# Ranks by odd counts, two sums moved to GpSimd, and a new order in a graph network kernel on one core

## The chip, the cores and the metric

The kernel runs on one core of a Trainium2 chip. The metric is the time of one execution on the device in microseconds (us). TensorE is called PE in the profile, its weight loads PEld, VectorE DVE, ScalarE ACT, GpSimd POOL and SyncE, whose queue issues the transfers, SP.

## The reference

There are 128 graphs of 128 nodes with 64 features, and a matrix `adj` of weights, most of them zero. Two layers follow each other; each adds its result to its input and normalizes over the features.

```
mask = adj > 0                                      # layer 0
diff = x[:, :, None, :] - x[:, None, :, :]
h    = relu((x @ W1a)[:, :, None, :] + diff @ W1b + b1)
hm   = einsum('bjkh,bjk->bjh', h, mask)             # 192 hidden features
deg  = sum(mask, -1)
x    = layernorm(x + hm @ W2 + deg * b2)

m    = relu(relu(x @ W1 + b1) @ W2 + b2)            # layer 1
msg  = relu(adj @ m)
gi, gh = msg @ W_ih.T + b_ih, x @ W_hh.T + b_hh     # three gates of 64
r, z = sigmoid(i_r + h_r), sigmoid(i_z + h_z)
n    = tanh(i_n + r * h_n)
x    = layernorm(x + (1 - z) * n + z * x)
```

The first layer's `hm` sums, for each node, a rectified vector over its neighbours only. A node has few neighbours, so the kernel gathers them.

## The kernel before, in words

The 128 graphs go through in 32 groups of four (`G = 4`). The nodes are in an order that spreads them over two halves of 64 (`K`). For each group the kernel does this:

- **Preparation** (`prep_parts`). `masks` (L410) compares the weights with zero on GpSimd. `ranks` (L416) counts, by a matmul of the mask with a triangle matrix `incl2`, how many marked nodes of the same half stand up to and with each node; L419 multiplies this by the mask on VectorE, so that marked nodes hold their rank 1, 2, 3 and so on, and all others 0. `degrees` and `counts` find how many neighbours a node has and how many extra segments of four (`W1`) it needs beyond the first eight (`W0`). `offsets` (L461, L462) makes `past` and `own`, which say which node owns which extra segment; `turned`, `owners` and `places` carry ranks over to the segments as `place`. `picks` (L518) compares `rankT` with 1 to 8 and `place` with 9 to 12, so that twelve one-hot matrices come out, `pick0` and `pick1`.
- **Values.** `values` multiplies the features by all projections at once; ScalarE copies the result to `uv` (L535). `pieces` splits a part of it into three bf16 pieces. `others` (L474) makes `t4`, the last 64 columns of `uv` times the degree plus `x`, by four VectorE instructions, one for each graph.
- **The main loop.** Each graph has six stretches, four of `pick0` and two of `pick1`, so 24 a group. In each, ScalarE writes the base value to a PSUM buffer `pv` (`seeds`, L581), TensorE adds the gathered values by 12 matmuls (`gathers`, L612), and VectorE sums absolute values into `part` (`reduces`, L628). There are three `pv` buffers. GpSimd adds up `part` (`together`, L650 to L657).
- **The tail** (`tail_parts`): the second matmul and `y0` with `t4` (L292), a normalization, the messages, the gates, the update and the second normalization, much of it on GpSimd.

Every part is a generator that stops between steps. The order is written out by hand: `TIMETABLE` gives each step a number, a group's numbers are shifted by `PER = 768` from the group before, and the steps are recorded in rising order of these numbers. `FIRST` and `SETUP` do this for the first group and the constants. The numbers are ranks in an order, not times. Each engine runs its instructions in the recorded order, and waits at each for what it needs; transfers stand in SP's queue in the same way. `uv`, `rankT` and most prepared tiles have two buffers, `t4` and `maskT` three, the loads four, and one pool of two PSUM buffers, `ps_w`, serves all matmuls but the gathers.

In `setup`, the tiles `gw1` and `gw2` get the second layer's weights on the diagonal of a cleared square. They are cleared by VectorE (L227) in the step that issues their transfers, which stands behind the main loop's first four reductions in the recorded order. The same step issues the transfers of the second layer's biases, which the next step of `setup` (L241 to L245) works on.

Of the kernel before, what the change touches and what calls it, by code (L numbers as in the profile page):

```python
# [12 lines left out]
ALU = mybir.AluOpType  # L13
# [15 lines left out]

PER = 768  # L30
TIMETABLE = {
    "load": (-1520,), "masks": (-771,), "ranks": (-470, -453), "degrees": (-560, -487), "turned": (-31, -23),
    "counts": (-196,), "offsets": (-3, 39, 50, 155, 157, 160, 160), "owners": (467, 555), "places": (193, 214),
    "pieces": (347, 412, 417, 418), "others": (-73, 422, 583, 1355), "values0": (-108, -102, -102),
    "values1": (136, 192, 192), "pick0": (-211, -102, 40, 69, 230, 278, 473, 532), "pick1": (579, 613, 613, 615),
    "over0": (263, 304), "over2": (461, 501), "base0": (-58,), "together0": (810, 990, 990, 1055),
    "sums0": (1213, 1219, 1219), "base1": (809,), "together1": (851, 1112, 1184, 1184), "base2": (594,),
    "together2": (1058, 1131, 1253, 1284), "sums2": (1328, 1348, 1383), "base3": (643,),
    "together3": (1240, 1256, 1316, 1326), "second": (1283, 1403, 1417, 1485, 1485, 1485), "turn": (1485, 1489),
    "message1": (1505, 1508), "message2": (1516, 1540), "message3": (1540, 1631),  # L40
    "gates": (1906, 1931, 1931, 1935, 1960, 1993), "update": (2192, 2539, 2962, 2962, 3012, 3044, 3156, 3920, 4537),
    "seed": (476, 511, 583, 612, 612, 661, 661, 686, 707, 721, 741, 806, 879, 923, 923, 973, 1019, 1065, 1073, 1156,
        1156, 1180, 1193, 1238),
    "gather": (487, 528, 589, 634, 649, 661, 703, 703, 734, 741, 760, 877, 907, 923, 946, 1002, 1034, 1069, 1131,
        1174, 1193, 1220, 1220, 1244),
    "reduce": (574, 574, 640, 647, 680, 706, 709, 736, 778, 803, 817, 914, 961, 1010, 1034, 1034, 1071, 1129, 1145,
        1176, 1214, 1237, 1276, 1322),
}


# [29 lines left out]
def adj_resnorm_kernel(  # L80
# [81 lines left out]
    def setup(ps_g, ps_w):  # L162
        def spread(t, src):
            nc.sync.dma_start(t, src.rearrange("(o n) -> o n", o=1).to_broadcast(list(t.shape)))

        for h in range(2):
            nc.sync.dma_start(wab[h * F : (h + 1) * F], w1.rearrange("(c f) h -> f c h", c=2))
        yield
        nc.vector.memset(bias, 0.0)
        nc.sync.dma_start(w2c, w2.rearrange("(c h) f -> h c f", c=2))  # L170
        for h in range(2):
            spread(bias[h * F : h * F + 3, 0:H], b1)
            spread(bias[h * F : h * F + 3, H:V], b2)
        nc.sync.dma_start(b1c, b1.rearrange("(c h) -> h c", c=2))
        make_identity(nc, ident)
        make_upper_triangular(nc, upper)
        nc.gpsimd.memset(nhalf, -0.5)
        nc.vector.memset(ones_h, 1.0)
        nc.vector.memset(zeros, 0.0)
        nc.vector.memset(halves, 0.0)  # L180
        for h in range(2):
            nc.vector.memset(halves[h * K : (h + 1) * K, h : h + 1], 1.0)
        nc.vector.tensor_copy(ident_h, ident)
        nc.vector.tensor_sub(strict, upper, ident)
        nc.vector.tensor_copy(incl2, upper)
        nc.vector.memset(incl2[0:K, K:N], 0.0)
        nc.vector.tensor_scalar_mul(strict_w, strict, -float(W1))
        nc.vector.tensor_copy(incl, upper)
        at = const.tile([N, 3], F32, name="at")
        nc.vector.tensor_add(at, ident[:, 0:3], ident[:, F : F + 3])  # L190

        for i in range(3):
            p = ps_g.tile([N, 2, 512], F32, tag="g", name="pv")
            for c in range(2):
                nc.tensor.matmul(p[:, c, :], ones_h, zeros, start=True, stop=True)
        ips = ps_w.tile([N, N], F32, tag="w", name="ips")
        nc.tensor.matmul(ips, ones_h, strict, start=True, stop=True)
        yield
        nc.vector.tensor_add(wall[:, 0:H], wab[:, 0, :], wab[:, 1, :])
        nc.vector.tensor_scalar_mul(wall[:, V : V + H], wab[:, 1, :], -1.0)  # L200
        nc.vector.tensor_copy(iota, ips)
        nc.vector.tensor_scalar_mul(w2c, w2c, 0.5)
        yield

        tps = ps_w.tile([HC, 4, F], F32, tag="w", name="tps")
        for c in range(4):
            cs = (V, V + HC, 0, HC)[c]
            nc.tensor.transpose(tps[:, c, :], wall[0:F, cs : cs + HC], ident[0:F, 0:F])
        nc.vector.tensor_copy(wT, tps.rearrange("p c (o f) -> p c o f", o=1).to_broadcast([HC, 4, 2, F]))
        yield  # L210
        dps = ps_w.tile([N, 2, F], F32, tag="w", name="dps")
        for d in range(2):
            for c in range(2):
                nc.tensor.matmul(dps[:, d, :], wT[:, 2 * d + c], w2c[:, c, :], start=c == 0, stop=c == 1)
        cps = ps_w.tile([N, F], F32, tag="w", name="cps")
        for c in range(2):
            nc.tensor.matmul(cps, b1c[:, c : c + 1].to_broadcast([HC, N]), w2c[:, c, :], start=c == 0, stop=c == 1)
        nc.vector.tensor_copy(wall[:, H:V], dps[:, 0, :])
        nc.vector.tensor_copy(wall[:, V + H : 4 * N], dps[:, 1, :])
        nc.vector.tensor_add(bias[:, H:V], bias[:, H:V], cps)  # L220
        yield
        piece = const.tile([N, NBI], BF16, name="piece")
        three_rows(slice(0, V), piece, at)
        yield

        for t, src in ((gw1, g_w1), (gw2, g_w2)):
            nc.vector.memset(t, 0.0)  # L227
            for h in range(2):
                nc.sync.dma_start(t[h * F : (h + 1) * F, h * F : (h + 1) * F], src)
        spread(bi, b_ih)  # L230
        spread(bias[:, V + F : V + 256], b_hh)
        spread(bias[:, V + 256 : NBI], g_b2)
        spread(b2bc, b2)
        for h in range(2):
            hs = slice(h * F, (h + 1) * F)
            nc.sync.dma_start(gb1[hs], g_b1.rearrange("(h o) -> h o", o=1))
            nc.sync.dma_start(wm[hs, 0:F], w_ihT[:, 128:H])
            nc.sync.dma_start(wm[hs, F:H], w_ihT[:, 0:128])
            nc.sync.dma_start(wx[hs, :], w_hhT)
        yield  # L240
        nc.vector.tensor_copy(bias[:, V : V + F], bi[:, 128:H])  # L241
        nc.vector.tensor_add(bias[:, V + F : V + H], bias[:, V + F : V + H], bi[:, 0:128])

        nc.vector.tensor_scalar_mul(bias[:, V + 256 : NBI], bias[:, V + 256 : NBI], 0.5)
        three_rows(slice(V, NBI), piece, at)  # L245
# [133 lines left out]
    with ExitStack() as fast:  # L379
# [25 lines left out]
        def prep_parts(s):  # L405
# [6 lines left out]

            def ranks():

                p = ps_w.tile([N, G, N], F32, tag="w", name=f"pc{g}")
                nc.tensor.matmul(p, incl2, s["maskT"], start=True, stop=True)  # L416
                yield
                s["rankT"] = prep.tile([N, G, N], BF16, tag="rankT", name=f"rankT{g}")
                nc.vector.tensor_mul(s["rankT"], p, s["maskT"])  # L419

            def degrees():
                p = ps_w.tile([N, G, 2], F32, tag="w", name=f"pd{g}")
# [8 lines left out]
            def counts():  # L431
# [5 lines left out]
                s["nseg"] = nseg_all[:, g * G : (g + 1) * G]  # L437
                nc.gpsimd.tensor_scalar(s["nseg"], rnd, BIGR, None, ALU.subtract)
                s["wseg"] = prep.tile([N, G], BF16, tag="wseg", name=f"wseg{g}")
                nc.gpsimd.tensor_scalar(s["wseg"], s["nseg"], float(W1), None, ALU.mult)  # L440
                tot = prep.tile([N, G], F32, tag="tot", name=f"tot{g}")
                nc.gpsimd.tensor_scalar(tot, s["nseg"], 2.0 * W1, 2.0 * W0, ALU.mult, ALU.add)
                s["npad"] = prep.tile([N, G], F32, tag="npad", name=f"npad{g}")
# [26 lines left out]
            def others():  # L470

                s["t4"] = prep.tile([N, G, F], F32, tag="t4", name=f"t4_{g}", bufs=3)
                for i in range(G):
                    nc.vector.scalar_tensor_tensor(  # L474
                        out=s["t4"][:, i, :], in0=s["uv"][:, i, V + H : 4 * N], scalar=s["deg"][:, i : i + 1],
                        in1=s["x"][:, i, :], op0=ALU.mult, op1=ALU.add,
                    )
                    yield

            def turned():  # L480

# [31 lines left out]
            def picks(t):  # L513
                def part():
                    name, n, src, first = ("pick1", W1, "place", W0 + 1) if t else ("pick0", W0, "rankT", 1)
                    s[name] = prep.tile([N, n, G, N], BF16, tag=name, name=f"{name}_{g}")
                    for i in range(n):
                        nc.vector.tensor_scalar(s[name][:, i], s[src], float(first + i), None, ALU.is_equal)  # L518
                        yield

                return part
# [320 lines left out]
```

## Time and profile before

| | |
|---|---|
| median of 3 runs | 1085.34 us (1084.07 to 1085.81) |
| the profiled execution | 1083.69 us |
| its span, from first to last instruction | 1081.8 us |
| its mean granted TensorE clock | 0.974 |
| busy: PE, PEld | 952.1, 778.3 us (88%, 72%) |
| busy: DVE, ACT, POOL | 992.6, 934.4, 840.4 us (92%, 86%, 78%) |
| longest groups: L628 on DVE; L581 on ACT (two forms); L612 on PE | 709.2; 409.3 and 206.3; 499.4 us |

In the table by stretches, a row holds the bounds of the stretch, its length, and for each of PE, PEld, DVE, ACT and POOL the busy time with the number of instructions; then the granted clock, the share of the DMA engines and their rate. A row of waits names an engine and line, what ended its waiting, the sum, how often, and the longest. A row of the timeline has start, duration, engine, line, operation and tiles; in brackets stands the idle time of the engine ahead of it and what ended it. Instructions of one engine overlap a little: one starts while the end of the one before is still written.

### The profile page before, as it was taken

How to read it: one execution, taken by the hardware profiler on the slowest of the kernel's cores; microseconds unless marked ns; L12 is line 12 of the kernel's file. 1: busy time of each engine (PE TensorE's matmuls, PEld its weight loads, DVE VectorE, ACT ScalarE, POOL GpSimd, SP SyncE). 2: the span in 40 equal slices, each digit the busy share in tenths (PEclk: the TensorE clock that was granted, in tenths of full speed). 3: DMA queues.
4: the chain of work that ended last, by engine and by line, in shares of the span. 5: the costliest groups of instructions: out<-in, count | busy, mean ns of one | idle time of the engine just before them, and what ended most of it. 6: DMA issues, size and time to landing. Idle time of an engine off the chain costs nothing.

```text
span 1081.8 us, 33583 instructions
## 1 busy us (share of the span) xinstructions
PE 952.1 (88%) x13432; PEld 778.3 (72%) x13432; DVE 992.6 (92%) x2352; ACT 934.4 (86%) x1576; POOL 840.4 (78%) x1227
## 2 busy tenths in 40 slices
PE   6588999999999999999999999999999998999882
PEld 4367777877777777777777777777777777777761
DVE  6598999999999999999999999999999999999971
ACT  3489999999999999999999999999999999999850
POOL 2266678888888888888888888888888888888766
PEclk9699999999999999999999999999999999999995
DMA  1200000000000000000000000000000000000000
GB/s 49 59 2 22 22 22 21 27 7 26 22 26 26 26 27 7 26 22 27 26 26 26 7 27 21 26 27 26 26 7 26 22 26 27 26 7 6 7 6 22
DMA packets 21368, 23.95 MB, mean 22 GB/s; under 512 B 4050, under 2 KB 17112, under 8 KB 21208
## 3 DMA queue, kind: packets, MB, share of 16 engines
q1 hardware_dynamic: 21208, 21.76, 6.7%
q8 instruction: 107, 1.75, 0.6%
q14 instruction: 53, 0.43, 0.1%
HBM read 17.55 MB, written 4.19 MB: 20 GB/s over the span
## 4 chain that ended last, share of the span: by engine, by line
PE 34%; POOL 25%; DVE 20%; ACT 16%; issue 3%; DMA 1%; SPq 0%; POOLq 0%; ACTq 0%; DVEq 0%
PE pv L612 16%; DVE part L628 13%; ACT pv L581 10%; PE pu L528 4%; POOL part L654 3%; POOL part L657 3%; ACT b L547 3%; POOL rs L275 2%; POOL part L650 2%; DVE pick L518 2%; PE pm L305 2%; PE pa L323 2%; POOL uc L365 2%; POOL ub L362 2%; POOL y L368 2%
## 5 line engine op out<-in xcount | busy, mean ns | idle before, releaser
L628 DVE TENSOR_REDUCE part<-pv 128x192 f32<-128x768 f32 x768 | 709.2, 946 | 21.8 <-PE pv L612 14.9
L612 PE MATMUL pv<-b,pick 64*128 64x192 bf16 x9216 | 499.4, 245 | 65.2 <-ACT pv L581 64.1
L612 PEld LDWEIGHTS <-pick 64*128 64x128 bf16 x9216 | 387.9, 94 | 155.3 <-issue 125.7
L581 ACT COPY pv<-uv 128x768 f32<-128x768 f32 x512 | 409.3, 809 | 37.7 <-DVE part L628 33.7
L581 ACT COPY pv<-us 128x768 f32<-128x768 f32 x256 | 206.3, 806 | 16.8 <-DVE part L628 10.3
L650 POOL TENSOR_TENSOR part<-part 128x384 f32<-128x384 f32 x128 | 127.8, 998 | 76.4 <-DVE part L628 76.2
L535 ACT COPY uv<-pu 128x512 f32<-128x512 f32 x128 | 68.6, 586 | 35.3 <-PE pu L531 35.3
L670 PE MATMUL ph<-ownT,part 128*96 128x128 f32 x512 | 88.3, 274 | 1.2 <-POOL part L657 1.2
L528 PE MATMUL pu<-wall,xT 64*128 64x512 f32 x256 | 86.8, 645 | 1.4 <-ACT off L454 1.2
L556 POOL TENSOR_TENSOR b<-r,b 128x1024 bf16<-128x1024 f32 (+1 forms) x35 | 68.8, 1965 | 20.7 <-ACT b L553 17.4
L518 DVE TENSOR_SCALAR pick<-rankT 128x512 bf16<-128x512 bf16 x256 | 84.1, 330 | 0.0
L654 POOL TENSOR_TENSOR part<-part 128x192 f32<-128x192 f32 x128 | 78.2, 611 | 2.5
L287 PE MATMUL pw<-w2c,hmT 96*128 96x64 f32 x512 | 78.2, 284 | 0.6 <-ACT hmT L676 0.5
L669 PE MATMUL ph<-ident,part 128*96 128x128 f32 x256 | 71.6, 280 | 7.0 <-ACT pv L581 6.7
L468 POOL CAST own<-own 128x512 f32<-128x512 bf16 x32 | 19.5, 610 | 74.5 <-DVE own L462 74.5
L657 POOL TENSOR_TENSOR part<-part 128x192 f32<-128x192 f32 x128 | 77.1, 602 | 0.0
L287 PEld LDWEIGHTS pw<-w2c,hmT 96*128 96x128 f32 x512 | 66.9, 190 | 10.8 <-ACT hmT L676 5.7
L652 POOL TENSOR_TENSOR part<-part 128x192 f32<-128x192 f32 x128 | 74.1, 590 | 0.0
L670 PEld LDWEIGHTS ph<-ownT,part 128*96 128x96 f32 x512 | 70.6, 166 | 2.7 <-POOL part L657 1.8
L275 POOL TENSOR_TENSOR rs<-ve,nhalf 128x4 f32<-128x4 f32 x64 | 66.5, 1039 | 5.3
L592 PE MATMUL pz<-uv,own 128*128 128x192 f32 x256 | 60.0, 358 | 9.4 <-DVE larger L429 9.4
L550 POOL TENSOR_TENSOR r<-uv,b 128x1024 f32<-128x1024 f32 x31 | 66.1, 2131 | 0.0
(137 smaller groups left out, 1626.3 us busy)
## 6 DMA issues: line engine op xcount, KB each, us to landing
adjT<-in_adjT_dram SPq DMA_DIRECT2D x32, 256.0 KB, 2.8
xT<-in_xT_dram SPq DMA_DIRECT2D x64, 64.0 KB, 2.6
x<-in_x_dram SPq DMA_DIRECT2D x32, 128.0 KB, 2.3
out_dram<-o SPq DMA_DIRECT2D x32, 128.0 KB, 1.7
wab<-in_w_dram SPq DMA_DIRECT2D x2, 96.0 KB, 2.5
bi<-in_b_ih_dram SPq DMA_DIRECT2D x1, 96.0 KB
bias<-in_b_hh_dram SPq DMA_DIRECT2D x1, 96.0 KB
wx<-in_w_hhT_dram SPq DMA_DIRECT2D x2, 48.0 KB, 3.5
```

Source lines behind the costliest of these rows:

```text
L275: nc.gpsimd.tensor_tensor(rs, ve, nhalf[:, 0:n], ALU.pow)
L287: nc.tensor.matmul(p[:, i, :], s["hmT"][:, i, c, :], w2c[:, c, :], start=c == 0, stop=False)
L518: nc.vector.tensor_scalar(s[name][:, i], s[src], float(first + i), None, ALU.is_equal)
L528: nc.tensor.matmul(ps[h], s["xT"][ks, i, :], wall[ks, :], start=True, stop=False)
L581: nc.scalar.copy(v, src.rearrange("p (c b h) -> p c b h", c=1, b=1).to_broadcast(list(v.shape)))
L612: nc.tensor.matmul(v[:, h, j, :], pick[ks, a + j, i, :], s[f"b{c}"][ks, i, F : F + H], start=False, stop=c == 2, skip_group_check=True,)
L628: nc.vector.tensor_reduce(into, view(s["pv", i, k]).rearrange("p c b h -> p h c b"), AX.XY, ALU.add, apply_absolute_value=True,)
L650: nc.gpsimd.tensor_tensor(f[:, 0:2], f[:, 0:2], f[:, 2:4], ALU.add)
L652: nc.gpsimd.tensor_tensor(f[:, 0], f[:, 0], f[:, 1], ALU.add)
L654: nc.gpsimd.tensor_tensor(f[:, 0], f[:, 0], f[:, no], ALU.subtract)
L657: nc.gpsimd.tensor_tensor(f[:, 0], f[:, 0], f[:, 1], ALU.add)
L670: nc.tensor.matmul(p[:, i, c, :], s["part1", i0 + i][:, 0, cs], s["ownT"][:, i0 + i, :], start=False, stop=True, skip_group_check=True,)
```

## The change

The triangle matrix gets 2 above the diagonal and 1 on it. The count of a marked node is then 2r - 1 for rank r, and that of any other node is even. So `rankT` needs no mask: ScalarE copies the counts, the picks compare with 1, 3, 5 and so on, and the constants that turn ranks into places are doubled. `others` makes `t4` of four graphs by two GpSimd instructions, a multiply with the degree spread over 64 columns and an add. `gw1` and `gw2` are cleared in the first step of `setup` with work on VectorE. The whole `TIMETABLE` is a new one; `PER`, `SETUP` and `FIRST` stay.

```diff
-    "load": (-1520,), "masks": (-771,), "ranks": (-470, -453), "degrees": (-560, -487), "turned": (-31, -23),
-    "counts": (-196,), "offsets": (-3, 39, 50, 155, 157, 160, 160), "owners": (467, 555), "places": (193, 214),
-    "pieces": (347, 412, 417, 418), "others": (-73, 422, 583, 1355), "values0": (-108, -102, -102),
+    "load": (-1520,), "masks": (-559,), "ranks": (-122, -122), "degrees": (-402, -367), "turned": (-19, -1),
+    "counts": (-114,), "offsets": (-22, -22, 80, 228, 245, 348, 349), "owners": (1039, 1066), "places": (368, 431),
+    "pieces": (337, 538, 550, 595), "others": (1085, 1194), "values0": (-55, -50, -37), "values1": (204, 204, 268),
...
-    "seed": (476, 511, 583, 612, 612, 661, 661, 686, 707, 721, 741, 806, 879, 923, 923, 973, 1019, 1065, 1073, 1156,
-        1156, 1180, 1193, 1238),
+    "seed": (644, 644, 657, 674, 684, 685, 711, 728, 728, 741, 761, 837, 923, 937, 978, 1149, 1149, 1173, 1203, 1221,
+        1271, 1326, 1395, 1397),
...
-        nc.vector.tensor_copy(incl2, upper)
+        nc.vector.scalar_tensor_tensor(out=incl2, in0=strict, scalar=2.0, in1=ident_h, op0=ALU.mult, op1=ALU.add)
         nc.vector.memset(incl2[0:K, K:N], 0.0)
-        nc.vector.tensor_scalar_mul(strict_w, strict, -float(W1))
+        nc.vector.tensor_scalar_mul(strict_w, strict, -2.0 * W1)
...
+        nc.vector.memset(gw1, 0.0)
+        nc.vector.memset(gw2, 0.0)
...
         for t, src in ((gw1, g_w1), (gw2, g_w2)):
-            nc.vector.memset(t, 0.0)
...
-                nc.vector.tensor_mul(s["rankT"], p, s["maskT"])
+                nc.scalar.copy(s["rankT"], p)
...
-                nc.gpsimd.tensor_scalar(s["wseg"], s["nseg"], float(W1), None, ALU.mult)
+                nc.gpsimd.tensor_scalar(s["wseg"], s["nseg"], 2.0 * W1, None, ALU.mult)
...
-                for i in range(G):
-                    nc.vector.scalar_tensor_tensor(
-                        out=s["t4"][:, i, :], in0=s["uv"][:, i, V + H : 4 * N], scalar=s["deg"][:, i : i + 1],
-                        in1=s["x"][:, i, :], op0=ALU.mult, op1=ALU.add,
-                    )
-                    yield
+                nc.gpsimd.tensor_tensor(s["t4"], s["uv"][:, :, V + H : 4 * N], wide(s["deg"], G), ALU.mult)
+                yield
+                nc.gpsimd.tensor_tensor(s["t4"], s["t4"], s["x"], ALU.add)
...
-                        nc.vector.tensor_scalar(s[name][:, i], s[src], float(first + i), None, ALU.is_equal)
+                        nc.vector.tensor_scalar(s[name][:, i], s[src], 2.0 * (first + i) - 1.0, None, ALU.is_equal)
```

## The prediction

> **What bounds the kernel now.** I read the table by stretches first, then the waits of the even part, then the timeline of one period, then the start.
>
> ```profile
> 0.00:54.00 54.00, 30.77 (x232) 20.93 (x234) 31.94 (x92) 21.95 (x42) 14.01 (x31) 0.78 0.20 54
> ...
> 540.00:648.00 108.00, 99.57 (x1440) 82.53 (x1439) 104.26 (x249) 99.04 (x167) 91.01 (x135) 1.00 0.07 22
> ```
>
> The columns are PE, PEld, DVE, ACT, POOL. The eight stretches from 108 to 972 us are alike: VectorE (DVE) is busy 834.6 of 864 us (96.6%), ScalarE (ACT) 796.2 (92.2%), TensorE (PE) 795.3 (92.0%), GpSimd (POOL) 713.7 (82.6%), at a granted clock of 1.00. The long L518 pick that ends each period starts at 499.69 and, four periods on, at 626.02: one group of four graphs takes 31.58 us. In these, DVE works 30.50, ACT 29.10, PE 29.07 and POOL 26.09. VectorE bounds, with 1.08 us idle, but two engines are only 1.4 us behind. The even part reaches from about 54 to 1026 us, 30.8 periods.
>
> The waits of 108 to 972 us (27.4 periods):
>
> ```profile
> ACT pv L581 <- DVE part L628: 33.9, 104, 0.7
> ACT uv L535 <- PE pu L531: 20.1, 28, 0.7
> ...
> DVE rh L350 <- ACT rz L348: 10.8, 27, 0.4
> ...
> DVE part L628 <- PE pv L612: 7.9, 26, 0.6
> ```
>
> ACT's 2.48 us of idle time in a period are 1.24 for a reduction that frees a `pv` buffer, 0.73 for the projection matmul, and 0.5 of small gaps. The three buffers of `pv` tie seed (ACT), gather (PE) and reduction (DVE) together, 24 times a period.
>
> **What VectorE loses.** Durations in a row overlap, so I take the distance from one start to the next.
>
> ```profile
> 504.02 0.67 DVE L419 TENSOR_TENSOR rankT<-pc,maskT 128x512 bf16<-128x512 f32 x1
> 504.61 1.80 DVE L628 TENSOR_REDUCE part<-pv 128x192 f32<-128x768 f32 x2
> ...
> 508.22 0.27 DVE L474 SCALAR_TENSOR_TENSOR t<-uv,deg,x 128x64 f32<-128x64 f32 x1
> 508.41 0.95 DVE L628 TENSOR_REDUCE part<-pv 128x192 f32<-128x768 f32 x1
> ```
>
> The product with the mask costs 0.59, one `t4` instruction 0.19, four 0.78 (the pair at 515.38 takes 0.39 to the next start). 30.50 - 0.59 - 0.78 = **29.13 us** for VectorE.
>
> **What ScalarE gains.** One copy of 128x512 out of PSUM, as `rank` is:
>
> ```profile
> 525.10 0.59 ACT L487 COPY rank<-pr 128x512 bf16<-128x512 bf16 x1
> 525.58 0.39 ACT L317 ACTIVATE m<-pn 128x256 f32<-128x256 f32 x1
> ```
>
> It costs 0.48: 29.10 + 0.48 = **29.58 us**, now the longest of the four. The f32 source bounds it: `place` (f32 to bf16) stands 0.64 from the next start. I take 0.48, the closer row, since the seed behind `place` may have waited. In the new order the count matmul stands right behind gather 23 on PE, and ACT reaches the copy after two seeds, which wait for reductions 21 and 22 (0.87 each), so the matmul (0.39) is hidden. If it is late, the copy holds all later seeds for up to one gather, 0.6 us a period.
>
> **What GpSimd gains.** A multiply with a broadcast operand (L281's form, 0.57 from start to start) and an add of two full ones (L368's, about 0.69): 26.09 + 1.26 = 27.35 us. Nothing waits early: the add stands some 280 of the 768 plan units (11 us) ahead of the `y0` that reads it, and the next load into `x`'s buffer, now freed by GpSimd, a further 360 units later. I cost the wait at nothing; without that cover it is at most 1.3 us a period.
>
> **New period.** ScalarE's 29.58 plus its waits. From below: only the projection wait goes on half as long, 0.35: 29.9. From above: all 2.48 of idle time stays: 32.06. VectorE's release of `pv` is now 0.45 us shorter per period than ScalarE's work and no longer the bound, but reductions still come in runs of three behind picks and statistics. I keep the projection's 0.73 (the first `uv` still stands right behind its matmul, which in the new order also needs the buffer that `mT` frees) and half of the 1.24: 29.58 + 0.73 + 0.62 = **30.93**, 0.65 less. Over 30.8 periods: **-20 us**.
>
> The odd counts and doubled constants change no operation's size; in setup a two-input instruction (0.35, as `own`) replaces a copy (0.22).
>
> **What the order moves.** Mask, counts and first picks of the next group come some 80 to 350 units later (a mask 559 units ahead of its group's zero instead of 771, the rank copy 122 instead of 453), and seeds, gathers and reductions some 170 later, so the distance from preparation to use stays about the same. SP issues the same 4 loads a group at the same place; their buffers' last readers stand hundreds of units ahead. The adding-up of `part`, 26.09 with all else on GpSimd, keeps its number of instructions. I cost these moves at nothing beyond the waits in the next sum; the rivals hold what they may cost.
>
> **The start.**
>
> ```profile
> 28.33 0.31 DVE L227 MEMSET gw<- 128x128 f32 x2
> 28.52 2.38 SPq L229 DMA_DIRECT2D gw<-in_g_w_dram  x4
> ...
> 34.31 0.19 DVE L241 COPY bias<-bi 128x64 f32<-128x64 f32 x1 [5.68 <-DMA bi<-in_b_ih_dram]
> 34.77 0.29 DVE L242 TENSOR_TENSOR bias<-bias,bi 128x128 f32<-128x128 f32 x1 [0.26 <-DMA bias<-in_b_hh_dram]
> ...
> 36.02 0.20 DVE L244 TENSOR_SCALAR bias<-bias 128x64 f32<-128x64 f32 x1 [0.96 <-DMA bias<-in_g_b_dram]
> ```
>
> Clearing the weights' tiles stands behind the fourth reduction in VectorE's order; SP's queue waits for it with the weight, bias and load transfers behind, and VectorE then waits for them. Moved up, the clearing fits into the 0.97 us in which VectorE waits for `wab`, and SP goes on at 9.0 us, as soon as its loads for group 1 are issued. The bias transfers start some 19 us earlier and are there. That removes 5.68 + 0.26 + 0.96 + 0.31 = 7.2 us. Late next is the first reduction behind setup: now it also waits 3.78 us for `pz`, `us`, `ownT` and a seed, and in the new order the second `pz` and `ownT` come later. I take half of that, 1.9: **-9 us**, between -6 and -12.
>
> **The end.** The page's last 56 us are a chain through group 31. In GpSimd's order `ve`, `rs` of group 30 (1.3 us) now stand behind group 31's `y`, not ahead of it, but with `yc` and an `o` still ahead of its last `rs`. I cost it at 0, within 1.5 either way.
>
> **Sum.** From the profiled execution, 1083.69 us (span 1081.8 and 1.9 around it): -20 - 9 gives 1054.7. The median shown, 1085.34, is 1.65 above it, so **1056**.
>
> **A rule that speaks against it.** VectorE's instructions are sometimes longer beside GpSimd's:
>
> ```profile
> 531.18 0.59 DVE L518 TENSOR_SCALAR pick<-rankT 128x512 bf16<-128x512 bf16 x1
> ...
> 1020.09 1.37 DVE L474 SCALAR_TENSOR_TENSOR t<-uv,deg,x 128x64 f32<-128x64 f32 x2
> ```
> ```profile
> 531.03 0.59 POOL L652 TENSOR_TENSOR part<-part 128x192 f32<-128x192 f32 x1
> ...
> 1020.07 0.73 POOL L365 TENSOR_TENSOR uc<-ub,tn 128x256 f32<-128x256 f32 x1
> ```
>
> A pick that is 0.28 elsewhere took 0.59 and ended 0.15 us after the GpSimd addition at its side (531.62); two `t4`, 0.47 elsewhere, took 1.37. So a collision costs 0.31 to 0.45, say 0.38. Today about one pick of twelve per period is hit, as 84.1 us for 256 against a median of 0.284 also says (11.4 us over 32 groups). `past` and `own` run at 0.25 and 0.35, mostly while GpSimd itself waits for `own`.
> The Trainium skill, SBUF — State Buffer, section Who interferes with whom, says that VectorE and GpSimd share a pair of ports under an exclusive lock, taken by fast-mode instructions and those with two SBUF inputs, and that the loser waits for the whole instruction. By that rule, the trace agrees for these two, and the new order, which spreads `past` and `own` beside GpSimd's mask (1.5 us), could pay it more often.
>
> **Rivals.**
> - *The lock eats it* (slower, 0.17). Twenty VectorE instructions of a period can collide (12 picks, 4 `past`, 4 `own`). With six more hits VectorE needs 29.13 + 6 x 0.38 = 31.4, and with today's 1.08 idle 32.5: +0.9 x 30.8 - 9 = +19, 1104. It decides from (1.37 + 9/30.8)/0.38 = 4.4 more hits a period on. For it: GpSimd goes from 83 to 88% of a period. Against: today's twenty-four candidates are hit about once.
> - *ScalarE runs almost without a gap* (0.18): 29.9, -1.68 x 30.8 = -52, with the start 1026. For it: VectorE's own idle time is only 1.08. Against: ScalarE waits on two partners.
> - *The order gives nothing* (0.12): three engines within 0.5 us of each other lose in waiting what VectorE saves; 31.58 stays and only the start counts: 1076. At its worst, with ScalarE's whole 2.48 (32.06), it is 1091; that part is what I count as no difference.
> - *The early clearing frees nothing* (0.05), if another wait holds SP's queue: 1065. The built program shows SP's first weight transfer waiting only for the clearing and an older load, so it is unlikely.
> - My forecast (0.48): periods of 30.4 to 31.4, 1038 to 1071.
>
> **Numbers.** Eight in ten: 1028 to 1092, which leaves out the best of the second rival and most of the first. A measurement of this kernel tells about 0.2% from no change: faster 0.78, within 0.2% 0.05, slower 0.17.
>
> **What would show it.** In the changed profile: ScalarE busiest in the even stretches (above 95%), VectorE about 94%; a period near 30.9; ScalarE's wait for reductions at half of 1.24; no DMA wait at the bias copies; picks still near 284 ns in the median. It is wrong if picks, `past` or `own` are often above 0.5 us, if the rank copy waits for its matmul, or if VectorE idles over 2 us for gathers.

## The result, and the profile after

The changed kernel takes **1053.40 us** (median of 4 runs, 1052.88 to 1053.97) where the kernel before takes 1085.57 (4 runs beside them): a ratio of 0.9702, 95% interval 0.9689 to 0.9715. Forecast were 1056 and faster. The total came out nearly; the table below shows that the gain of the periods was forecast 2.7 us too high and the gain of the start 2.7 us too low, so that the two errors cancelled.

Each group has one `y0` (L292 before, L293 after), so its 32 starts are a clock that counts groups. First and last `y0` in the timelines of VectorE, of the kernel before:

```profile
76.25 0.41 DVE L292 TENSOR_TENSOR y<-pw,t 128x256 f32<-128x256 f32 x1
...
1053.56 0.42 DVE L292 TENSOR_TENSOR y<-pw,t 128x256 f32<-128x256 f32 x1 [4.42 <-PE pw L685]
```

and of the changed kernel:

```profile
64.56 0.42 DVE L293 TENSOR_TENSOR y<-pw,t 128x256 f32<-128x256 f32 x1
...
1024.57 0.42 DVE L293 TENSOR_TENSOR y<-pw,t 128x256 f32<-128x256 f32 x1 [4.15 <-PE pw L684]
```

They split the gain of the span (1081.8 to 1051.9, 29.9 us) into its three places:

| | before | after | difference | forecast |
|---|---|---|---|---|
| up to the first `y0` | 76.25 | 64.56 | -11.7 | -9 |
| 31 periods between first and last | 977.3, 31.53 each | 960.0, 30.97 each | -17.3 | -20 |
| from the last `y0` to the end | 28.2 | 27.3 | -0.9 | 0 |

In the even part, the table by stretches (columns PE, PEld, DVE, ACT, POOL) has for the changed kernel:

```profile
0.00:54.00 54.00, 37.85 (x357) 26.12 (x358) 41.72 (x109) 32.01 (x56) 21.62 (x42) 0.87 0.20 54
...
540.00:648.00 108.00, 101.45 (x1462) 81.81 (x1460) 103.38 (x238) 102.39 (x175) 96.05 (x137) 1.00 0.10 26
```

From 108 to 972 us, 27.9 periods, VectorE (DVE) is busy 829.1 of 864 us (96.0%), 29.72 of a period of 30.97, ScalarE (ACT) 816.8 (94.5%) or 29.28, TensorE (PE) 29.06, GpSimd (POOL) 27.54. In the first 54 us VectorE now does 41.7 us of work, against 31.9 before. The waits of the same 864 us:

```profile
ACT pv L580 <- DVE part L627: 21.8, 56, 0.4
ACT uv L534 <- PE pu L530: 14.5, 28, 0.5
...
DVE part L627 <- PE pv L611: 11.3, 27, 0.4
...
DVE rh L351 <- ACT rz L349: 5.4, 27, 0.2
```

ScalarE waits 0.78 us a period for reductions (1.24 before) and 0.52 for the projection (0.73 before). VectorE waits 0.40 for gathers (0.29 before) and 0.19 for the gates (0.39 before). The groups of the picks and of the rank copy:

```profile
L517 DVE TENSOR_SCALAR pick<-rankT 128x512 bf16<-128x512 bf16 x256 | 88.7, 367 | 1.5 <-ACT rankT L421 1.5
...
L421 ACT CAST rankT<-pc 128x512 bf16<-128x512 f32 x32 | 18.6, 580 | 6.5 <-PE pc L418 6.5
```

The rank copy waited for its matmul twice, at 7.46 us for 5.4 and at 30.82 us for 1.1, and never in the even part. The two `t4` steps on GpSimd take 0.61 and 0.73 us and waited for nothing. The picks grew from a mean of 330 ns to 367.

At the start, the weights' transfers leave SP at 9.16 us instead of 28.52, and the bias work on VectorE waits for nothing:

```profile
9.16 2.39 SPq L230 DMA_DIRECT2D gw<-in_g_w_dram  x4
```
```profile
28.20 0.26 DVE L242 COPY bias<-bi 128x64 f32<-128x64 f32 x1
...
33.41 1.92 DVE L627 TENSOR_REDUCE part<-pv 128x192 f32<-128x768 f32 x2 [0.47 <-PE pv L611]
```

### The profile page after: what moved, and what is told of

Read it like the earlier page. It is cut to its first block, busy times and chain, and to the rows that moved or that the text cites. A ratio compares the mean times of both kernels' runs of the same rounds, so it can differ in the third digit from the quotient of the medians.

```text
span 1051.9 us, 33435 instructions
## 1 busy us (share of the span) xinstructions
PE 952.7 (91%) x13432; PEld 762.5 (72%) x13432; DVE 968.2 (92%) x2192; ACT 943.2 (90%) x1608; POOL 883.3 (84%) x1291
## 3 DMA queue, kind: packets, MB, share of 16 engines
q8 instruction: 107, 1.75, 0.7%
## 4 chain that ended last, share of the span: by engine, by line
POOL 37%; DVE 29%; ACT 14%; PE 12%; issue 8%; DMA 0%; SPq 0%; POOLq 0%; DVEq 0%; ACTq 0%
DVE part L627 15%; ACT pv L580 7%; POOL part L649 6%; POOL part L653 4%; POOL part L656 4%; PE pv L611 4%; DVE pick L517 4%; POOL r L549 4%; POOL part L651 4%; POOL b L555 3%; DVE own L464 3%; DVE stats L269 2%; POOL yc L279 2%; POOL ua L360 2%; POOL rs L276 2%
## 5 line engine op out<-in xcount | busy, mean ns | idle before, releaser
L627 DVE TENSOR_REDUCE part<-pv 128x192 f32<-128x768 f32 x768 | 699.3, 948 | 32.0 <-PE pv L611 17.5
L649 POOL TENSOR_TENSOR part<-part 128x384 f32<-128x384 f32 x128 | 127.9, 999 | 19.1 <-DVE part L627 17.3
L534 ACT COPY uv<-pu 128x512 f32<-128x512 f32 x128 | 75.1, 587 | 27.7 <-PE pu L530 23.5
L527 PE MATMUL pu<-wall,xT 64*128 64x512 f32 x256 | 92.0, 637 | 1.6 <-ACT off L456 1.2
L517 DVE TENSOR_SCALAR pick<-rankT 128x512 bf16<-128x512 bf16 x256 | 88.7, 367 | 1.5 <-ACT rankT L421 1.5
L288 PE MATMUL pw<-w2c,hmT 96*128 96x64 f32 x512 | 75.1, 278 | 0.5 <-ACT hmT L675 0.5
L288 PEld LDWEIGHTS pw<-w2c,hmT 96*128 96x128 f32 x512 | 69.7, 191 | 6.6 <-issue 4.9
```

The lines of the kernel that those rows point to most:

```text
L288: nc.tensor.matmul(p[:, i, :], s["hmT"][:, i, c, :], w2c[:, c, :], start=c == 0, stop=False)
L517: nc.vector.tensor_scalar(s[name][:, i], s[src], 2.0 * (first + i) - 1.0, None, ALU.is_equal)
L627: nc.vector.tensor_reduce(into, view(s["pv", i, k]).rearrange("p c b h -> p h c b"), AX.XY, ALU.add, apply_absolute_value=True,)
L649: nc.gpsimd.tensor_tensor(f[:, 0:2], f[:, 0:2], f[:, 2:4], ALU.add)
```

## The experiments

The theory after the result: the start and the order each give their part, VectorE's lost work is worth less than its size because three engines are close, and collisions of VectorE with GpSimd take back some of it. The rivals: the order alone does everything, GpSimd's added work costs something, or the collisions are the bound.

### The start: early clearing in the old order, and late clearing in the new one

```diff
+        nc.vector.memset(gw1, 0.0)
+        nc.vector.memset(gw2, 0.0)
...
-            nc.vector.memset(t, 0.0)
```

> The kernel before with one part of the change: gw1 and gw2 cleared early. If the stall of VectorE at the bias copies is lost time (7.2 us, and some of the 3.8 us behind it), the time falls by 7 to 9 us, to about 1077, and the even period stays 31.6 us. The rival: the first period only shifts its waits, since the next reductions wait for PE and ScalarE anyway; then it falls by less than 3 us.

Measured: 1079.43 us (ratio 0.9935, 0.9914 to 0.9957), 6.0 us less than before. Its first `y0` starts at 69.36, 6.9 us earlier; 0.9 is lost again on the way (in the profiled execution the periods are 31.63 us where they were 31.53). That is a little under the expected gain.

The other way round, the changed kernel with the two clearings back in the step that issues the transfers:

> The changed kernel with the clearing back behind the fourth reduction. If the stall at the start is lost time, 7 to 9 us come back: 1060 to 1063. If the new order's first period is held by something else, it stays at 1054 to 1056.

Measured: 1060.82 us (ratio 0.9771, 0.9752 to 0.9790), 7.4 us more than the changed kernel, with the first `y0` at 71.03, 6.5 us later. So the clearing is worth 6 to 7.4 us under either order: the 7.2 us of removed stall, and nothing more. The other 4.8 us up to the first `y0` (11.7 - 6.9) come with the new order: with both operations back on VectorE in it (the run of 1149.04 us below) the first `y0` still stands at 65.1, 4.3 ahead of 69.36. With early clearing in the old order VectorE's first reduction behind `setup` still waits:

```profile
38.41 0.96 DVE L629 TENSOR_REDUCE part<-pv 128x192 f32<-128x768 f32 x1 [3.78 <-PE pv L613]
```

In the changed kernel this reduction stands at 33.41 and waited 0.47 us (above). The 3.78 us, of which I let half go, went almost wholly; the other 1.5 of the 4.8 us I did not locate.

### The new operations in the old order

The changed kernel with the `TIMETABLE` of before, and `"others": (422, 583)` for the two steps of `t4`:

> The changed kernel with the old timetable (the two t4 steps at 422 and 583). If the relief of VectorE is what counts, whatever the order, the period falls here too, to 30.6 to 31.2 us, and the time to 1050 to 1066. If the new order is what makes use of the relief, the period stays at 31.4 or more and the time at 1071 to 1077, the early clearing's gain alone. If the shared port eats it, picks, past and own are often above 0.5 us and the time is above 1080.

Measured: **1147.34 us** (ratio 1.0569, 1.0550 to 1.0588), far above the first two expectations. The third, above 1080 by collisions, has the direction but not the sign that it named: `past` and `own` keep their 251 and 352 ns, and only the picks grew, from a mean of 332 ns with early clearing alone to 391. In the old order the moved operations cost 68 us (against 1079.43). In its trace the rank copy stands in ScalarE's line between `us` and `b0`, and VectorE waits 24.4 us for the gates (L351). I took that for the cause. Two kernels test it, each with one of the two moved operations only, both in the old order with early clearing. First the odd counts and the rank copy, with `t4` on VectorE in its four old places:

```diff
-                nc.vector.tensor_mul(s["rankT"], p, s["maskT"])
+                nc.scalar.copy(s["rankT"], p)
```

> The kernel before with the early clearing and with odd counts and the rank copy on ScalarE; t4 stays on VectorE in its four old places. The old order with all operations moved gave 1147.34 us, against 1079.43 with the early clearing alone. Theory A (the rank copy is what the old order cannot take: it waits for its matrix product ahead of b0 in ScalarE's line, and the gates behind it come late): 1120 to 1150 us here, and the partner run with t4 alone moved stays at 1070 to 1090. Theory B (t4 on GpSimd is the cause): 1065 to 1085 here, 1120 to 1150 there. Both in parts: each between 1085 and 1120.

Measured: 1089.24 us (ratio 1.0044, 1.0028 to 1.0061). VectorE waits for the gates as long as in that run, 25.5 us, but the price is 9.8 us, not 68. Then `t4` on GpSimd alone, the rank product on VectorE:

> The kernel before with the early clearing and with t4 on GpSimd in two steps at 422 and 583 of the old order; the rank product stays on VectorE. Theory A (the rank copy on ScalarE was the cause of 1147.34): 1070 to 1090 us, about the early clearing's 1079 or a little less, for 0.8 us less VectorE work in a period. Theory B (GpSimd's own steps late, and picks stretched beside them): 1120 to 1150 us.

Measured: 1138.62 us (ratio 1.0505, 1.0476 to 1.0534), 59.2 more than 1079.43. My reading of the trace falls: `t4` is most of it, and 9.8 + 59.2 = 69.0 account for the 67.9. The waits from 108 to 950 us of this kernel name another place, beside 26.9 us in TensorE's weight loads for `x`:

```profile
PE pt L299 <- POOL x L282: 21.2, 25, 0.9
ACT x1T L302 <- PE pt L299: 20.7, 23, 1.1
```

and its timeline shows GpSimd's line around `x`:

```profile
501.91 0.72 POOL L477 TENSOR_TENSOR t<-t,x 128x256 f32<-128x256 f32 x1
...
505.52 0.23 POOL L274 TENSOR_SCALAR ve<-mv 128x4 f32<-128x4 f32 x1
...
507.53 0.61 POOL L282 TENSOR_TENSOR x<-yc,rs 128x256 f32<-128x256 f32 x1
```

The second `t4` step stands ahead of the update and of the normalization that ends in `x`. The statistics for `ve` are there at 504.4, but GpSimd comes to it at 505.52. `x` ends 5.08 us after the start of `y0` (503.06); with early clearing alone it is 4.15 (511.44 to 515.59). TensorE's transpose and ScalarE's `x1T` wait for `x`, and the seeds behind `x1T` with them. To test that, both steps are put behind `x` and the mask, with nothing else changed:

```diff
-    "others": (422, 583)
+    "others": (830, 830)
```

> As the run of 1138.62 us (the kernel before with the early clearing, t4 on GpSimd, the rank product on VectorE), with one thing changed: both t4 steps stand at 830 of the old order instead of 422 and 583, so they come behind x and maskT in GpSimd's line instead of ahead of ub, uc, y and x. Theory (the loss of 59 us against 1079.43 came from x, which left GpSimd some 1.4 us later, and with it the transposes pt, ScalarE's x1T and everything queued behind x1T on ScalarE): the waits for x at L299 fall from 26.9 and 21.2 us to under 10 and about 0, and the time is 1068 to 1084 us. Rival (the old order has no room for t4 on GpSimd anywhere, for GpSimd's line or for the stretched picks): 1110 to 1140.

Measured: **1083.80 us** (ratio 0.9984, 0.9974 to 0.9994), inside the expected range at its upper end. The same instructions on the same engine, further on in its line, are 55 us cheaper. So the place in GpSimd's line is what `t4` cost. The 26.9 us are 5.4, and TensorE's matmuls and `x1T` have no such wait any more:

```profile
PEld pt L299 <- POOL x L282: 5.4, 26, 0.3
```

The same edit did a second thing, which the run does not separate from the first: the picks of `rankT`, 84.6 us in all with early clearing alone, were stretched to 106.3 with `t4` at the old places and are back at 85.5. How the 55 us divide between the wait for `x`, the stretched picks and the lower clock (last section) is therefore not shown.

It is still 4.4 us slower than with `t4` on VectorE in the same order, so in the old order neither move gains anything.

### The old operations in the new order

The rank product back on VectorE, the rest as changed:

```diff
-                nc.scalar.copy(s["rankT"], p)
+                nc.vector.tensor_mul(s["rankT"], p, s["maskT"])
```

> The changed kernel with the rank back on VectorE as a product with the mask, in the new order. If VectorE bounds the period (29.7 us busy of 31.0 in the changed kernel), its 0.59 us comes back whole: 18 us, 1071. If ScalarE or a mix of engines bounds it, VectorE has 1.2 us to spare and ScalarE gets 0.48 us back: 1045 to 1058.

Measured: 1060.11 us (ratio 0.9765, 0.9746 to 0.9783), 6.7 more than the changed kernel, between the two expectations. First and last `y0` (64.39 and 1030.91) give a period of 31.18, 0.21 more. VectorE's 0.59 us are worth a third of their size; that is a net price, since ScalarE loses the copy in the same edit.

`t4` back on VectorE, two instructions at each of the two new places (1085 and 1194):

> The changed kernel with t4 back on VectorE, two instructions in each of the two steps, in the new order. If VectorE bounds the period, its 0.78 us comes back: 24 us, 1077, and more where a t4 stands beside a GpSimd instruction (0.38 us each). If a mix of engines bounds it, at most half: 1054 to 1066.

Measured: **1149.56 us** (ratio 1.0587, 1.0565 to 1.0609), 96 more. With both operations back on VectorE it is the same:

> The new order and the early clearing, with the rank product and t4 both on VectorE. If the relief is what counts and VectorE bounds, 1.37 us a period come back: 1095, so this order is worse for the old work than the old one (1077 with the early clearing). If the order is what counts, it stays near 1060.

Measured: 1149.04 us (ratio 1.0587, 1.0566 to 1.0609). So the rank product adds nothing to this price, and four instructions of 0.19 us are not 3.1 us a period by their work. In the first of the two kernels the mean of one is 813 ns. Its two pairs in the timeline, and what GpSimd does beside the second:

```profile
526.14 0.47 DVE L476 SCALAR_TENSOR_TENSOR t<-uv,deg,x 128x64 f32<-128x64 f32 x2
...
531.10 2.80 DVE L476 SCALAR_TENSOR_TENSOR t<-uv,deg,x 128x64 f32<-128x64 f32 x2
```
```profile
531.69 2.12 POOL L553 TENSOR_TENSOR r<-uv,b 128x1024 f32<-128x1024 f32 x1
```

The pair at 526.14 ran while GpSimd waited for `own`, and took 0.47. The pair at 531.10 ended at 533.90, right behind `r` (533.81): its second instruction took 2.16 us, standing still through the whole of `r`, and its first 0.72, through the addition of 0.59 us ahead of `r` (531.14 to 531.73). That is the collision of the prediction, at 2.33 us instead of 0.38. The test: all four instructions at the harmless one of the two places.

```diff
-    "others": (1085, 1194)
+    "others": (1085, 1085)
```

> The changed kernel with the four t4 operations back on VectorE, but all four at the first of their two places (time 1085 of the order), where GpSimd stands idle until own is ready; nothing else differs from the run that gave 1149.56 us, in which the second pair took 2.80 us beside GpSimd's r. Theory (the price of the pair is the collision with r, not its work): the pair takes about 0.47 us there, VectorE gets 4 x 0.2 = 0.8 us more work in a period than in the changed kernel, and the time is 1054 to 1079 us. Rival (the new order fits only a VectorE without t4, wherever it stands): 1130 to 1150 us.

Measured: **1061.46 us** (ratio 0.9782, 0.9765 to 0.9798), as expected, and 88 less than with the second place. Four instructions take 0.86 us there:

```profile
515.26 0.86 DVE L476 SCALAR_TENSOR_TENSOR t<-uv,deg,x 128x64 f32<-128x64 f32 x4
```

So `t4` on VectorE costs 8.1 us in the new order if it is well placed. First and last `y0` (64.81 and 1033.01) give a period of 31.23, 0.26 more for 0.78 us of work: again a third, here with GpSimd's two instructions gone at the same time.

### GpSimd's added work, and the collisions that are left

Here `t4` is simply `x`: the degree term is left out, and with it both GpSimd instructions.

```diff
-                nc.gpsimd.tensor_tensor(s["t4"], s["uv"][:, :, V + H : 4 * N], wide(s["deg"], G), ALU.mult)
-                yield
-                nc.gpsimd.tensor_tensor(s["t4"], s["t4"], s["x"], ALU.add)
+                s["t4"] = s["x"]
```

> The changed kernel without the degree term: t4 is x itself, so the two GpSimd instructions are left out and nothing takes their place. If GpSimd's added 1.3 us a period are hidden, the time stays within 2 us of 1053.4. If GpSimd or the shared port holds the period, it falls by up to 1.3 x 30.8 = 40 us, to 1013; 5 to 15 us would mean a part of it.

Measured: 1052.45 us (ratio 0.9697, 0.9677 to 0.9717). Without the 1.3 us of GpSimd's work it is 1.0 us shorter, which the intervals do not tell from nothing: hidden, as forecast.

In the changed kernel three picks of each period run beside GpSimd's instructions. VectorE's and GpSimd's rows of the timeline:

```profile
502.81 0.55 DVE L517 TENSOR_SCALAR pick<-rankT 128x512 bf16<-128x512 bf16 x1
...
505.99 0.56 DVE L517 TENSOR_SCALAR pick<-rankT 128x512 bf16<-128x512 bf16 x1
...
506.75 0.35 DVE L464 SCALAR_TENSOR_TENSOR own<-iota,off,past 128x128 bf16<-128x128 bf16 x1
```
```profile
502.60 0.62 POOL L279 TENSOR_TENSOR yc<-y,mv 128x256 f32<-128x256 f32 x1
...
505.79 1.51 POOL L411 TENSOR_SCALAR maskT<-adjT 128x512 bf16<-128x512 f32 x1
```

The two picks shown and a third at 507.02, of 0.43, are 0.27, 0.28 and 0.15 over the usual 0.28, together 0.70 us. Moved away:

```diff
-    "pick0": (-44, 50, 88, 133, 133, 137, 251, 419)
+    "pick0": (-60, -60, 133, 133, 133, 137, 251, 419)
```

> The changed kernel with its first three picks moved in the order, from -44, 50 and 88 to -60, -60 and 133, so that they run beside GpSimd's short pow on 4 elements or beside nothing, and no longer beside yc and maskT, where they took 0.55, 0.56 and 0.43 us instead of 0.28. Theory (these three collisions cost 0.70 us of VectorE's period, and VectorE bounds, with GpSimd's line starting at own, which then comes 0.7 us earlier): period 30.3, time 1032 to 1040 us. Mixed bound (as the rank product's 0.59 us was worth 0.22 us): 1043 to 1050. Rival (the picks are stretched wherever they stand, or GpSimd alone bounds from a later point): 1052 to 1055, and a sum of picks near 88 us again.

Measured: 1053.15 us (ratio 0.9713, 0.9693 to 0.9733): no change, although the edit did what it should:

```profile
L517 DVE TENSOR_SCALAR pick<-rankT 128x512 bf16<-128x512 bf16 x256 | 69.3, 312 | 1.5 <-ACT rankT L421 1.5
```

The group of picks is 19.4 us shorter (88.7 above), VectorE is busy 798.3 us from 108 to 950 us where it was busy 807.9, and the period is 30.97 as ahead of the edit. What VectorE saved became waiting, in the same stretch: 12.9 us for gathers where it was 10.9, and 5.8 us in which `past` now waits for ScalarE's `off`. The time is that of the rival, but not its reason: the picks are not stretched wherever they stand. The test has one flaw: a pick moved from 50 to -60 now stands ahead of the first `past` (-22), so the edit shifted the steps behind it too. Within that, the theory that these three collisions are a cost in this kernel falls.

## Why the prediction was right, and where it was not

**The period: 30.93 forecast and 30.97 measured, which is luck in part.** I had VectorE at 29.13 us of work and ScalarE, at 29.58, as the new bound at over 95%. Measured are 29.72 and 29.28: VectorE is still the busiest (96.0%, where I had 94), ScalarE is at 94.5%. The sum 29.58 + 0.73 + 0.62 has two errors. ScalarE's work is 0.30 too high in it, and the 0.5 us of small gaps that I had read from the kernel before is left out without a reason. With the measured numbers the same three terms give 29.28 + 0.52 + 0.78 = 30.58, 0.39 short of the period, and these 0.39 are the small gaps. A period of 30.93 by this sum says nothing on whether ScalarE bounds.

**The work of an engine: "30.50 - 0.59 - 0.78 = 29.13" failed, and so did "29.10 + 0.48".** VectorE's busy time fell by 0.78 us instead of 1.37, ScalarE's grew by 0.18 instead of 0.48. Such a sum takes out or adds an instruction and leaves the others alone, but busy time counts overlapping instructions once, and the overlap changed. Counted in the trace over 27 whole periods, each instruction from the end of the one ahead of it, VectorE's picks take 0.31 us a period more (three collisions in place of one) and its 24 reductions 0.36 more, together about the missing 0.6. A single reduction lasts as long as before (948 ns against 946), but six in a period now come after a gap where it was two, and an instruction after a gap overlaps nothing. On ScalarE it is the other way round: the copy adds 0.51, and the 24 seeds take 0.41 less, since three in a period come after a gap where it was nine.

**My signs.** Picks above 0.5 us were to show that the forecast is wrong; two of the twelve in each period are (0.55 and 0.56), though the median stayed at 285 ns, and they turned out to cost nothing that the experiment could measure. The rank copy has no wait in the even part, and VectorE idles 0.40 us a period for gathers, under the 2 that I named. In the recorded rivals the 1026 of the second should be 1025 by its own terms (1085.34 - 1.68 x 30.8 - 9); nothing hangs on it.

**What bounds now: not VectorE's work alone, and what else stays open.** Four kernels in the new order, VectorE's busy time in a period against the period:

| kernel | VectorE's work | period |
|---|---|---|
| picks moved | 29.4 | 30.97 |
| as changed | 29.7 | 30.97 |
| rank product on VectorE | 30.2 | 31.18 |
| `t4` on VectorE, well placed | 30.4 | 31.23 |

In the one run below 29.7 less work for VectorE is worth nothing; above it a microsecond is worth about 0.4, in runs that each take work from another engine too. GpSimd's `t4` is worth nothing either. No run took work from TensorE, or from ScalarE alone, so which of them or which chain through several engines makes the 31.0 stays open. The chain that ended last does not settle it: in the changed kernel it runs for 37% of the span through GpSimd and for 29% through VectorE, and with the picks moved, at the same period, for 35% through TensorE and 26% through ScalarE.

**The waits: the projection's went down, the reductions' by less than half.** 0.73 became 0.52, where I had kept it; 1.24 became 0.78, where I had taken 0.62. Together 1.30 against 1.35.

**The start: 11.7 against 9.** The stall's term held: 7.2 forecast, 6.0 to 7.4 by the two runs. The term "I take half of that, 1.9" was mis-sized: the new order gave 4.8, with the wait of 3.78 down to 0.47. The other error, of the periods, is that 0.65 a period was forecast and 0.56 came: the marks put the period before at 31.53, not 31.58, and the new one at 30.97.

**The end: 0 against 0.9.** Inside the 1.5 either way.

**The rival of the lock was the nearest miss.** It was given 0.17 and is real: it cost 88 us in the kernel that differs from a good one only by a pair of instructions at another place. It was told with the wrong instructions and the wrong price. I counted hits of `past`, `own` and picks at 0.38. In the changed kernel these are cheap, and the expensive partner is GpSimd's `r` of 2.12 us beside an instruction with two inputs. The change escapes it because `t4` left VectorE. The Trainium skill, SBUF — State Buffer, section Who interferes with whom, says that a VectorE instruction with two SBUF inputs contends with a GpSimd instruction that reads SBUF, and that the port pair they share is an exclusive lock. For the pair of `t4` the trace agrees: 2.80 us, to the end of `r`. For the mask it does not: a pick that began 0.20 us into the 1.51 us of `maskT` ended 0.75 us ahead of its end, and `own`, with two inputs, ran at its usual 0.35 beside it; only the pick after it (507.02, 0.43 us) ended 0.15 us behind the mask. Here the measurement decides: not every GpSimd instruction holds VectorE up for its whole length.

**The order: "I cost these moves at nothing" was wrong as a way to see it.** In the old order the moved operations cost 68 us; adding up the single prices, all but 14 of them are for two places in GpSimd's line (9.8 for the rank copy and 4.4 for `t4` well placed remain). In the new order the old operations take 1149 us, most of it for one place of a pair. With both operations on VectorE and `t4` well placed, the two prices of 6.7 and 8.1 added to 1053.4 give 1068 (an estimate, this kernel was not run), 11 less than the old order with early clearing. By that estimate the order brings 11 us by itself and lets the operations bring 15; in the old order they bring nothing.

## What to carry to other kernels

Where several engines are within 5% of each other, price a moved instruction by its neighbours in the line and its partner on the next engine, not by its duration: the same `t4` cost 4 or 59 us on GpSimd in one order and 8 or 96 on VectorE in the other, by place alone. Look first whether it now stands ahead of a step that starts another engine's chain, and, between VectorE and GpSimd, whether it runs beside a long instruction of the other. Do not take an engine's busy time as a sum of its instructions: it also changes with how often they come after a gap. Marks that occur once in each iteration (here `y0`) split a gain into start, period and end, and show when a good total hides two wrong terms.

## What the runs showed of the hardware that I had not expected

**A wait of TensorE of about 2 us can cost another 1.7 us in clock, by where it falls.** The four kernels of 1138 to 1149 us have a granted clock of 0.97 or 0.98 from 108 to 950 us; the others, from 1052 to 1089 us, have 1.00. The timeline of TensorE with `t4` on GpSimd in the old order shows two waits close together:

```profile
506.60 0.67 PE L611 MATMUL pv<-b,pick 64*128 64x192 bf16 x12 [0.85 <-ACT pv L580]
508.20 0.54 PE L299 MATMUL pt<-ident,x 128*128 128x128 f32 x2 [0.92 <-POOL x L282]
508.67 1.14 PE L611 MATMUL pv<-b,pick 64*128 64x192 bf16 x12
```

Behind them, twelve matmuls of a gather take 1.14 us instead of 0.67. In the table by stretches, here of 3.41 us, TensorE's busy time is the first column behind the length and the clock the third from the end of a row. The last two rows are from two periods later:

```profile
504.99:508.40 3.41, 1.64 (x31) 1.18 (x25) 3.41 (x6) 2.75 (x5) 3.16 (x6) 1.00 0.11 38
508.40:511.81 3.41, 3.41 (x28) 2.23 (x28) 1.68 (x9) 1.89 (x4) 2.75 (x3) 0.50 0.00 0
...
573.25:576.67 3.42, 1.96 (x35) 1.46 (x33) 3.29 (x5) 2.89 (x5) 3.17 (x6) 1.00 0.13 43
576.67:580.08 3.41, 3.37 (x45) 2.52 (x47) 2.90 (x11) 2.75 (x6) 2.99 (x3) 1.00 0.00 0
```

The clock is halved for 3.41 us, which is 1.71 us of full speed missing. This does not happen in every period, but in 14 of the 25 from 108 to 950 us. In the clock's records of this kernel the halved stretches begin 34.13 us apart or a multiple of 3.41 us more (133.12 us), while its period is 33.38 us: they keep to a raster of 3.41 us that runs on by itself. In the four kernels together there are 53 of them, and in the stretch of the raster ahead of each TensorE was busy for 0.33 to 0.53 of the time. The least busy stretch that no halved one followed had 0.51, 0.52, 0.43 and 0.44 in the four kernels, and 0.54 or more in the others. So what counts here is whether the waits fall into one stretch of the raster and leave TensorE busy for less than about half of it. With `t4` on VectorE in the new order, a wait of 2.09 us ahead of the gather at 535.65 fell into one stretch, busy 1.39 us of 3.42, and the clock was halved behind it; the same wait of 2.09 ahead of the gather at 570.05 was divided between two stretches, busy 1.65 and 2.50 us, and the clock stayed at 1.00.

The mean clock says how much of the loss this can be: 0.957 of 1131.8 us against 0.978 of 1082.8 with the two steps behind `x`, 48.7 us missing against 23.8, so 25 of the 49 us between the two profiled executions, if a microsecond of clock is one of time, which no run shows. Estimated for a period, the delay of 0.93 us in `x` and 14 x 1.71 us spread over 25 periods (0.96) make 1.9; measured is 1.75 (33.38 by first and last `y0`, against 31.63). The Trainium skill, TensorE: Matmul & The Clock Gate, section Part 1: The HAM clock gate, says that the clock is at half speed after an idle window of about 3.4 us. The trace agrees with the 3.4. The window need not be idle here: TensorE was busy for a third to a half of it.
